# Where the zeros in the unwritten corners of a causal score tile come from: TensorE or ScalarE

## The chip, the cores and the metric

The kernel runs on one core of one Trainium2 chip. The metric is the device time of one execution in microseconds; lower is better. Times come from repeated runs, and views of the profile from one profiled execution of the same kernel.

## The reference, cut to what matters

The reference is a chain of four blocks on x of shape (2, 512, 256), all in float32: causal attention with rotary embedding and 16 heads of 128, a feed-forward block with dequantised weights, a linear attention and a second feed-forward block with weights from a table. The change lies in the first:

```python
attn = jnp.einsum('bihd,bjhd->bhij', q, k) * scale
causal = jnp.triu(jnp.ones((s, s), dtype=bool), k=1)
attn = jnp.where(causal[None, None], -jnp.inf, attn)
attn = jax.nn.softmax(attn, axis=-1)
o = jnp.einsum('bhij,bjhd->bihd', attn, v).reshape(b, s, N_HEADS * D_K)
```

Row i of a head's 512x512 scores has only columns 0 to i. Two sequences of 16 heads make 32 heads.

## The kernel before, in words

**Engines and order.** All instructions of an engine are issued in the order in which the program writes them; the kernel schedules itself. A small planner (`Times` and `Engine`, lines 48 to 187) keeps a model of when each engine is free and when each tile is written. It decides only where side work goes: chains of small steps (`begin` and `poll`, lines 245 to 262), which run whenever TensorE's modelled time `now` has come far enough, and fillers for VectorE (`fill`, line 134). Every operation that goes through `scalar`, `vector`, `pool` or `sync` is recorded at line 183 (DMAs at 165), so the profile shows these lines for nearly everything; tiles tell operations apart. Matrix products go through `matmul` (line 276), which from the first head on cuts an output of 128 rows into two products of 64 rows, one for each half of the array (line 281). Each float32 product leaves two records in the trace, one bfloat16 product one.

**A slot for each head.** `slot(i)` (line 1090) writes, in this order: the scores of head i; the projections of q and k for head i+1; on ScalarE the division of head i's probabilities by their sums; the output projection of head i-2 (`projected_out`); the product of probabilities and values of head i-1 (`attended`, line 983); the turning of head i's probabilities (VectorE transposes and four DMAs into pT, `turned_p`); a part of a later head's values. In the last slots the first feed-forward block takes the place of projections that are no longer needed.

**The scores of a head.** Four tiles of 128 rows, each in two halves of 64 rows (`score_half`, line 933). A half has as many columns as its last row needs, so that the lower half of a tile has 64 columns less than the upper one. Tile 3 (448 and 512 columns) fills a bank of PSUM with the tag "s", tiles 2 and 0 share the next "s" bank, tile 1 (256 and 192 columns) is in a bank with the tag "t". Each tag has two banks, taken in turn (`bank`, line 233). VectorE then reads a whole tile of 128 rows at once with the mask (`scores`, line 911). In tiles 3 and 1 a corner of 64 rows by 64 columns is read that no score is written to: rows 0 to 63 and columns 448 to 511 of tile 3, rows 64 to 127 and columns 192 to 255 of tile 1. The mask makes its values irrelevant, but they must be finite. In tiles 2 and 0 the corners are laid out so that each is a score of the other tile or covered.

**Zeros for the two corners.** `no_scores` (line 949) writes a corner with one bfloat16 product of zeros, 64 columns of weights by 64 columns, taken from the left part of the mask, which is zero. It is called at line 1129, between tile 3 and tile 2, and at line 1145, between the two halves of tile 1.

**The banks of tag "t"** hold tile 1 of a head and `po`, the output of `attended`, which ScalarE then copies with the bias of v to oT (line 996).

Of the kernel before, what the change touches and what calls it, by code (L numbers as in the profile page):

```python
# [19 lines left out]
P = 128  # L20
HALF = P // 2
B = 2
S = 512
# [11 lines left out]
TU = HT * P  # L35
# [155 lines left out]
def sandwich_kernel(  # L191
# [36 lines left out]
    vector, scalar = Engine("DVE", nc.vector, times), Engine("ACT", nc.scalar, times)  # L228
# [4 lines left out]
    def bank(tag):  # L233
        tile = psum.tile([P, 512], F32, tag=tag, name=f"ps_{tag}")
        used = banks.setdefault(tag, deque(maxlen=2))
        if len(used) == 2:
            times.floor[tile.name] = times.end(used[0])
        used.append(tile.name)
        return tile
# [9 lines left out]
    def begin(chain, delay=0.0):  # L249
        chains.append([now[0] + delay, chain])  # L250
# [13 lines left out]
    def catch_up():  # L264
        if behind:
            behind.popleft()()
# [9 lines left out]
    def matmul(out, lhsT, rhs, start, stop, beside=False, **more):  # L276
        m = lhsT.shape[-1]
        step = HALF if halved[0] else P
        for at in range(0, m, step):
            part = slice(at, min(at + step, m))  # L280
            nc.tensor.matmul(out[part], lhsT=lhsT[:, part], rhs=rhs, start=start, stop=stop, **more)  # L281
        now[0] = max(now[0], times.start("PE", [out], [lhsT, rhs]))
        if not beside:
            now[0] += (math.prod(rhs.shape[1:]) / 0.6 + 5) / 1e3
        times.add("PE", now[0], [out], [lhsT, rhs])
# [21 lines left out]
    def col(kind, i):  # L307
        at = {"q": 0, "k": NH, "v": 2 * NH, "g": 3 * NH, "b": 3 * NH + NK}[kind] + i
        return cols_sb[:, at : at + 1]
# [200 lines left out]
    with ExitStack() as at:  # L510
# [57 lines left out]
        mask = ac.tile([P, S + P], F32, name="mask")  # L568
# [259 lines left out]
        NS = B * NH  # L828
# [79 lines left out]
        def blocks(t, n):  # L908
            return t.rearrange("p (b c) -> p b c", c=n)
# [39 lines left out]
        def no_scores(ps):  # L949

            nc.tensor.matmul(ps, lhsT=zeros, rhs=zeros, start=True, stop=True)  # L951

        def exps(i, it):
            p, mn = ps_p[i]
            pi = p[:, p_at[it] : p_at[it] + (it + 1) * P]
            scalar.activation(
                pi,
                pi,
                AF.Exp,
                bias=mn[:, it : it + 1],  # L960
                scale=-1.0,
                accum_out=sums[i][:, it : it + 1],
            )
# [19 lines left out]
        def attended(i):  # L983
            gg, hh = divmod(i, HG)
            po = bank("t")
            for jt in range(NT):
                matmul(
                    po[:, jt * P :],
                    vs[gg][:, jt, hh * DK : (hh + 1) * DK],
                    pT[i][:, :, 4 * jt : 10 + jt : 3, :].rearrange("p i t b -> p t i b"),  # L990
                    jt == 0,
                    jt == NT - 1,
                )
            oT[i] = vp.tile([P, S], F32, tag="oT", name="oT")

            scalar.activation(oT[i], po, AF.Identity, bias=col("v", i % NH))
# [21 lines left out]
        def attention_sums(b):  # L1018
            for t2 in range(NT // 2):
                h = acc[:, 2 * t2 : 2 * t2 + 2, :].rearrange("p t d -> p (t d)")  # L1020
                vector.tensor_add(h, h, yb[b][t2])
# [68 lines left out]
        def slot(i):  # L1090
            b, h = divmod(i, NH)
            g2, odd = divmod(i, HG)
            if i == 0:
                load("q", 2)
            elif i == 2:
                load("k", 2)
            if odd == 0:
                load("v", g2 + 2)
                load("o", g2)
            elif i > 1:  # L1100
                load("q", (i + 3) // 2)
                load("k", (i + 3) // 2)
            if i == 4:
                vector.tensor_tensor(differ, words[:, :, 0], words[:, :, 1], ALU.bitwise_xor)
            if i == NH + 2:
                attention_sums(0)
                begin(after_attention(0))
            if i == NH + 1:

                flat = [  # L1110
                    [t.rearrange("p k c -> p (k c)") for t in (up_i, wu)],
                    [t[0].rearrange("p k s -> p (k s)") for t in (xT0, xTv)],
                ]
                parts = [[t[:, at : at + TU] for at in range(0, t.shape[-1], TU)] for t in flat[1]]
                select_in(
                    parts[0] + parts[1],
                    [tuple(t[:, at : at + TU] for t in flat[0]) for at in range(0, NK * FULL * P, TU)],
                )
            now_in, done = i < NS, not (jobs or behind)
            if now_in:  # L1120
                ps_p[i] = (
                    pr.tile([P, 1280], F32, tag="p", name="p"),
                    small.tile([P, NT], F32, tag="mn", name="mn"),
                )
                sums[i] = small.tile([P, NT], F32, tag="sm", name="sm")
                s3 = bank("s")
                score_half(i, 3, 0, blocks(s3[:, : S - HALF], HALF))
                score_half(i, 3, 1, blocks(s3, HALF))
                no_scores(s3[:HALF, S - HALF :])
                scores(i, 3, blocks(s3, P))  # L1130


                s2 = bank("s")
                ps2 = s2[:, HALF : HALF + 3 * P]
                ps0 = blocks(s2, P)[:, 0:4:3, :HALF]
                score_half(i, 2, 1, blocks(ps2, HALF))
                score_half(i, 2, 0, blocks(ps2[:, : 2 * P + HALF], HALF))
                score_half(i, 0, 0, ps0[:, :1])
                score_half(i, 0, 1, ps0)
                scores(i, 2, blocks(ps2, P))  # L1140
                exps(i, 3)
                scores(i, 0, ps0)
                s1 = bank("t")
                score_half(i, 1, 1, blocks(s1[:, :TU], HALF))
                no_scores(s1[HALF:, TU - HALF : TU])
                score_half(i, 1, 0, blocks(s1[:, : TU - HALF], HALF))
                scores(i, 1, blocks(s1[:, :TU], P))
                exps(i, 2)
                exps(i, 0)
                exps(i, 1)  # L1150
            catch_up()
            if i < NS - 2:
                look_up(i > 0)
            else:
                assert not terms
            turning = []
            for kind in "qk":
                if kind == "q" and i in (0, 2, 3):
                    pass
                elif i + 1 < NS:  # L1160
                    turning.append(projection(kind, i + 1))
                    next(turning[-1])
                    next(turning[-1])
                elif i <= NS:
                    next(main)
                    next(main)
                if kind == "q" and jobs and i % 2 == 0 and i >= 2:
                    dequantised(*jobs.popleft())
                if kind == "q" and i and now_in:
                    inverted(i)  # L1170
            for work in turning:
                next(work, None)
            if now_in:
                p, _ = ps_p[i]
                for it in reversed(range(NT)):
                    pi = p[:, p_at[it] : p_at[it] + (it + 1) * P]
                    scalar.mul(pi, pi, rs[i][:, it : it + 1])
            if 2 <= i < NS + 2:
                projected_out(i - 2)
            if i == 0:  # L1180
                values(0, 1, "t")
            elif i == 1:
                values(1, 1, "t")
            if i in (1, 2):

                ahead = projection("q", i + 2)
                next(ahead)
            if 1 <= i < NS + 1:
                attended(i - 1)
            if i == 0:  # L1190
                values(1, 0)
            if now_in:
                turned_p(i)
            if i in (1, 2):
                for _ in ahead:
                    pass
            poll()
            if i < NS - HG:
                if i > 1:
                    values(i // 2 + 1, odd)  # L1200
            elif i <= NS:
                next(main)
                next(main)
            poll()
            if i < NS - 2:
                look_up(done)
            catch_up()
# [27 lines left out]
        for i in range(NS + 2):  # L1235
            slot(i)
# [313 lines left out]
```

## Time and profile before

| | |
|---|---|
| Median of three runs | 621.93 us (621.89 to 622.28) |
| Profiled execution | 622.14 us |
| its span in the profile | 620.0 us |
| Granted TensorE clock | 1.000 |
| Heads' part of the span (first scores to last scores) | 14.7 to 355.7 us |
| From one head's scores to the next, heads 12 to 30 | 11.04 us |
| Products of zeros | 64 |
| ScalarE busy | 299.6 us, 48% |

The span runs from the first to the last recorded instruction; the execution's own time holds some 2 us around it. PE is TensorE's products and PEld its weight loads, DVE is VectorE, ACT ScalarE, POOL GpSimd, SP SyncE, whose queue issues the DMAs. A row of a group gives the line, the engine, the operation, output and inputs, the shape and how often; then busy time, the mean of one, and the idle time of the engine before them. A row of a timeline gives start, duration, the same names, and how many instructions are merged. `128*64` in a row of TensorE means weights with 64 columns, an output of 64 rows. A product's row includes the time in which its result still runs through the array, so rows of products that follow each other overlap.

### The profile page before, as it was taken

The page shows a single profiled execution, that of the slowest core. Times are in us where ns is not written, and L with a number is a line of the kernel's source. Part 1 is how long each engine was busy: PE and PEld are TensorE (multiplying, and loading weights), DVE is VectorE, ACT ScalarE, POOL GpSimd, SP SyncE. Part 2 cuts the span into 40 slices and gives each one's busy share as a digit, 9 for nine tenths or more (in the row PEclk, how much of TensorE's full clock was granted, in tenths as well). Part 3 has the DMA queues.
Part 4 walks back from the last instruction along what each step waited for, and adds up shares of the span by engine and source line. Part 5 has one row for each costly group of instructions (what it writes and reads, how often), then busy time and mean ns, then how long its engine had stood idle before and what let it go on. Part 6 is the DMA issues. An engine that isn't in the chain of part 4 may idle for free.

```text
span 620.0 us, 13144 instructions
## 1 busy us (share of the span) xinstructions
PE 613.4 (99%) x4938; PEld 433.8 (70%) x4938; DVE 484.1 (78%) x1159; ACT 299.6 (48%) x659; POOL 275.5 (44%) x353
## 2 busy tenths in 40 slices
PE   8999999999999999999999999999999999999996
PEld 6555655555555666667777788888888888886676
DVE  6989988887887999989898888768977562563953
ACT  5646666775556556566556741233232323335130
POOL 5355657354453575755667300440360260261441
PEclk9999999999999999999999999999999999999999
DMA  8567474765547647556452521211000001001010
GB/s 220 143 165 213 105 199 124 170 167 142 162 123 177 169 114 185 154 140 179 110 142 58 131 54 28 108 34 29 2 18 18 2 10 26 1 4 34 19 35 17
DMA packets 43599, 60.90 MB, mean 98 GB/s; under 512 B 5136, under 2 KB 31504, under 8 KB 43536
## 3 DMA queue, kind: packets, MB, share of 16 engines
q1 hardware_dynamic: 43536, 60.07, 37.4%
q8 instruction: 39, 0.64, 0.4%
q14 instruction: 24, 0.20, 0.1%
HBM read 28.33 MB, written 1.05 MB: 47 GB/s over the span
## 4 chain that ended last, share of the span: by engine, by line
PE 98%; DVE 1%; issue 0%; DMA 0%; POOL 0%; ACT 0%; POOLq 0%; DVEq 0%
PE ps_mm L281 40%; PE ps_o L281 22%; PE ps_s L281 21%; PE ps_t L281 15%; DMA x<-in_x 0%; DVE st L183 0%; PE ps_t L288 0%; DVE hT L183 0%; POOLq L1546 0%; POOL rstd L183 0%; DVE mv L183 0%; ACT xT L183 0%; DVE x L183 0%; PE ps_s L288 0%; ACT wu L183 0%
## 5 line engine op out<-in xcount | busy, mean ns | idle before, releaser
L183 DVE SCALAR_TENSOR_TENSOR rr<-ps_mm,cols_sb,sin_sb 64x512 f32<-64x512 f32 (+1 forms) x126 | 93.4, 741 | 3.7 <-PE ps_mm L281 0.9
L183 POOL TENSOR_TENSOR wg<-wg,scratch 128x752 f32<-128x752 f32 x30 | 53.8, 1792 | 90.6 <-DVE scratch L183 88.0
L281 PE MATMUL ps_mm<-xT,wg 128*64 128x256 f32 (+2 forms) x680 | 86.8, 379 | 0.0
L281 PE MATMUL ps_s<-xT,wu 128*64 128x256 f32 (+1 forms) x652 | 82.9, 379 | 0.0
L183 ACT ACTIVATE p<-p,mn 128x512 f32<-128x512 f32 (+3 forms) x128 | 70.3, 550 | 24.6 <-DVE mn L183 24.4
L281 PE MATMUL ps_o<-wd,hT 128*64 128x256 f32 (+2 forms) x680 | 78.5, 376 | 0.0
L281 PE MATMUL ps_t<-pT,v 128*64 128x256 f32 (+3 forms) x512 | 75.5, 433 | 0.0
L281 PEld LDWEIGHTS ps_o<-wd,hT 128*64 128x64 f32 (+1 forms) x680 | 63.0, 141 | 13.2
L281 PEld LDWEIGHTS ps_mm<-xT,wg 128*64 128x64 f32 (+2 forms) x680 | 62.7, 139 | 12.9 <-ACT si L183 0.3
L281 PEld LDWEIGHTS ps_s<-xT,wu 128*64 128x64 f32 (+1 forms) x652 | 60.5, 139 | 12.1 <-DVE hT L183 0.3
L281 PEld LDWEIGHTS ps_t<-pT,v 128*64 128x64 f32 x512 | 45.4, 137 | 31.3 <-issue 22.6
L183 ACT ACTIVATE p<-p,rs 128x512 f32<-128x512 f32 (+3 forms) x128 | 61.4, 551 | 9.7 <-DVE rs L183 7.8
L281 PE MATMUL ps_o<-wo,oT 128*64 128x256 f32 x512 | 61.8, 379 | 0.0
L281 PEld LDWEIGHTS ps_o<-wo,oT 128*64 128x64 f32 x512 | 45.4, 137 | 22.2 <-issue 14.0
L281 PE MATMUL ps_mm<-xT,wq 128*64 128x512 f32 (+2 forms) x252 | 59.8, 583 | 0.4 <-ACT xT L183 0.4
L183 POOL TENSOR_TENSOR ra<-ra,cos_sb 128x512 f32<-128x512 f32 (+1 forms) x33 | 41.0, 1244 | 41.7 <-ACT ra L183 39.1
L281 PE MATMUL ps_mm<-xT,wk 128*64 128x512 f32 x248 | 59.5, 592 | 0.0
L281 PE MATMUL ps_s<-kT,qT 128*64 128x384 f32 (+5 forms) x384 | 57.7, 427 | 0.1
L281 PE MATMUL ps_mm<-wv,xTv 128*64 128x256 f32 x464 | 56.0, 379 | 0.0
L183 DVE STREAM_TRANSPOSE turned<-p 128x512 f32<-128x512 f32 (+3 forms) x128 | 54.1, 480 | 1.9 <-DMA pT<-turned 0.6
L183 ACT ACTIVATE ln<-x,shift,rstd 128x256 f32<-128x256 f32 x24 | 14.9, 626 | 76.7 <-POOL shift L183 76.7
L183 DVE CUSTOM_DVE_ANT_0 p<-ps_s,mask 128x512 f32<-128x512 f32 x64 | 31.1, 486 | 23.1 <-PE ps_s L951 23.1
(155 smaller groups left out, 957.7 us busy)
## 6 DMA issues: line engine op xcount, KB each, us to landing
pT<-turned SPq DMA_DIRECT2D x128, 208.0 KB, 3.9
wo<-in_wo SPq DMA_DIRECT2D x17, 256.0 KB, 4.0
wv<-in_wv SPq DMA_DIRECT2D x16, 256.0 KB, 4.0
wq<-in_wq SPq DMA_DIRECT2D x15, 256.0 KB, 4.7
wk<-in_wk SPq DMA_DIRECT2D x15, 256.0 KB, 4.5
xT<-tr SPq DMA_DIRECT2D x44, 64.0 KB, 2.2
pk_g<-in_gate_p SPq DMA_DIRECT2D x4, 256.0 KB, 4.3
sc_g<-in_gate_s SPq DMA_DIRECT2D x8, 128.0 KB, 4.0
```

What stands on the lines that cost most here:

```text
L183: return write(*args, **more)
L281: nc.tensor.matmul(out[part], lhsT=lhsT[:, part], rhs=rhs, start=start, stop=stop, **more)
```

## The change

For heads 2 to 30 the two products of zeros are left out. Instead a new function `prepare` takes the head's first "s" bank and its "t" bank early, in the slot before, and ScalarE copies zeros from the mask into the two corners. It is called from `attended`, behind its products and ahead of ScalarE's oT: `attended(i)` is written in slot i+1 and prepares head i+2. Heads 0, 1 and 31 keep the products. Since each bank is the next that its tag would give, the banks of all tiles are the same as before.

```diff
+        prepared = {}
+
+        def prepare(i):
+
+            prepared[i] = bank("s"), bank("t")
+            for rows, cs, ps in (
+                (slice(0, HALF), slice(S - HALF, S), prepared[i][0]),
+                (slice(HALF, P), slice(TU - HALF, TU), prepared[i][1]),
+            ):
+                scalar.copy(ps[rows, cs], mask[rows, :HALF])
+
@@ attended
+
+            if i + 2 < NS - 1:
+                prepare(i + 2)
             oT[i] = vp.tile([P, S], F32, tag="oT", name="oT")
 
             scalar.activation(oT[i], po, AF.Identity, bias=col("v", i % NH))
@@ slot
-                s3 = bank("s")
+                ready = prepared.pop(i, None)
+                s3 = ready[0] if ready else bank("s")
                 score_half(i, 3, 0, blocks(s3[:, : S - HALF], HALF))
                 score_half(i, 3, 1, blocks(s3, HALF))
-                no_scores(s3[:HALF, S - HALF :])
+                if not ready:
+                    no_scores(s3[:HALF, S - HALF :])
                 scores(i, 3, blocks(s3, P))
...
-                s1 = bank("t")
+                s1 = ready[1] if ready else bank("t")
                 score_half(i, 1, 1, blocks(s1[:, :TU], HALF))
-                no_scores(s1[HALF:, TU - HALF : TU])
+                if not ready:
+                    no_scores(s1[HALF:, TU - HALF : TU])
                 score_half(i, 1, 0, blocks(s1[:, : TU - HALF], HALF))
                 scores(i, 1, blocks(s1[:, :TU], P))
```

The planner records the copies as work of ScalarE, as it does every operation; the products of zeros it did not count. So the places that it chooses for side work behind the heads can change too.

## The prediction, made before the changed kernel was run

> **What bounds the kernel now.** I read the page's busy line and the chain that ended last first, then the groups of TensorE by shape, then the timeline of one head on TensorE and on ScalarE, and last the end of TensorE's timeline.
>
> ```profile
> span 620.0 us, 13144 instructions
> ...
> PE 613.4 (99%) x4938; PEld 433.8 (70%) x4938; DVE 484.1 (78%) x1159; ACT 299.6 (48%) x659; POOL 275.5 (44%) x353
> ...
> PE 98%; DVE 1%; issue 0%; DMA 0%; POOL 0%; ACT 0%; POOLq 0%; DVEq 0%
> ```
>
> TensorE is busy in 99% of the span and is 98% of the chain. The view of waits has it waiting for other engines only in the first microseconds (1.0, 0.4 and 0.2 us). Its clock is granted in full. So what leaves TensorE's queue shortens the kernel, and what other engines get costs only if TensorE comes to wait for it.
>
> The groups by shape (columns: count, busy us, mean ns of one, idle):
>
> ```profile
> L281 PE MATMUL ps_s<-kT,qT 128*64 128x384 f32 x64 | 26.9, 501 | 0.1
> L281 PE MATMUL ps_s<-kT,qT 128*64 128x320 f32 x64 | 22.5, 433 | 0.0
> ...
> L281 PE MATMUL ps_t<-kT,qT 128*64 128x256 f32 x64 | 19.1, 380 | 0.0
> L281 PE MATMUL ps_t<-kT,qT 128*64 128x192 f32 x64 | 16.6, 341 | 0.0
> ...
> L951 PE MATMUL ps_t<-mask 128*64 128x64 bf16 x32 | 6.2, 193 | 0.0
> L951 PE MATMUL ps_s<-mask 128*64 128x64 bf16 x32 | 6.2, 192 | 0.0
> ```
>
> The zeros are 64 products of 193 ns, 12.4 us in the busy column, but that is not their price: products overlap. One row lasts about 167 ns plus its columns: 433 for 320 and 380 for 256 differ by 53 ns for 64 columns, 0.83 ns a column. The price is the distance between starts. Two shapes break the line: 384 columns should take 433 + 53 = 486 and take 501; 192 should take 380 - 53 = 327 and take 341. These two follow a product of zeros. Each float32 product leaves two records, and only the first comes right behind the zeros, so 14.5 ns in the mean is 29 ns in that one.
>
> One head, TensorE (start, duration):
>
> ```profile
> 141.91 1.02 PE L281 MATMUL ps_s<-kT,qT 128*64 128x512 f32 x4
> 142.66 0.19 PE L951 MATMUL ps_s<-mask 128*64 128x64 bf16 x1
> 142.69 0.99 PE L281 MATMUL ps_s<-kT,qT 128*64 128x384 f32 x8
> 143.48 0.38 PE L281 MATMUL ps_t<-kT,qT 128*64 128x256 f32 x1
> 143.52 0.19 PE L951 MATMUL ps_t<-mask 128*64 128x64 bf16 x1
> 143.55 0.53 PE L281 MATMUL ps_t<-kT,qT 128*64 128x192 f32 x3
> 143.90 1.89 PE L281 MATMUL ps_mm<-xT,wq 128*64 128x512 f32 x8
> ```
>
> Products of 64 output rows go side by side into two halves of the array. The scores of this head last from 141.906 to 143.904 (the trace's own starts), 1.998 us; all heads 2 to 30 show 1.998 to 2.004. The lower half has 448+384+64+256 columns, the upper 512+320+128+192: 1152 each, twice, at 0.833 ns: 1.920 us, and some 2.5 ns for each of eight products: 1.940. The excess is 0.058 us, and each half has one product of zeros. So neither half hides the other's.
>
> **What it removes.** Behind the last 448 columns the zeros start at 142.662 and the next product at 142.690: 28 ns. That product's weights began to load only when the zeros began (142.664), the load behind it began at 142.720, and so its own took 56 ns, of which the zeros covered 28; the rest is the 29 ns seen in the groups. In the other half it is the same (143.521, 143.549, 143.579). Price: 28 + 29 = 57 ns in each half, once in a head, halves in parallel. The Trainium skill (TensorE: Matmul & The Clock Gate, "Wait — 56ns, not 53.3ns?") speaks against this much: a small matmul costs its floor, start to start about 25 ns. By that a head gains 25 ns and 29 heads 0.73 us, lost within what can be told from no change; by the rows it is more than twice that, because the floor leaves out the weight load that a 28 ns product is too short to cover. I take the rows, as the excess of 58 ns confirms them. The function that prepares is called for heads 2 to 30, 29 heads (0, 1 and 31 keep the products): 29 x 57 = 1.65 us, all on the path.
>
> **What it adds on ScalarE.** Two copies of 64x64 in 29 heads. The nearest row is the copy of v, 128x512 at 585 ns; less 448 columns at 0.83 it is 212 ns. Bounds: 187 ns, the engine's smallest row (reading an accumulator), and 387 ns, the scaling of 128x128. Two take 0.42 us by my value, 0.37 to 0.77 by the bounds. They stand behind the four scalings of p and ahead of oT:
>
> ```profile
> 137.82 1.92 ACT L183 ACTIVATE p<-p,rs 128x512 f32<-128x512 f32 x4 [0.55 <-DVE rs L183]
> 140.40 0.69 ACT L183 ACTIVATE oT<-ps_t,cols_sb 128x512 f32<-128x512 f32 x1 [0.66 <-PE ps_t L281]
> ```
>
> ScalarE sits idle ahead of oT for 0.63 to 1.3 us in nearly every head from 4 on (0.41 in head 20). So the copies fill that hole; at 0.77 us oT would be 0.1 us late in every second head, and oT is read only in the next slot, behind its scores and projections; the copy of v behind oT has a hole of its own (1.04 us here). No cost. Without that cover 0.42 us would go into the exponentials, whose products have room too: in this head pT lands at 146.60 and is read at 149.06; the room is 1.4 us in the first three heads and 2.3 or more after.
>
> **The new waits.** The first product of scores of a head waits for the first copy. The scalings end 1.88 to 4.1 us before that product in all these heads (139.74 to 141.91 here), so 0.42 us of copies leave 1.4 us or more. The banks rotate as before, and the copies wait for no other engine in the build. In front of the product of 256 columns the build puts one more semaphore instruction on TensorE's queue; nothing but the rest of the scores and q's projection is queued behind it. Two such instructions in a row start 111 ns apart (146.510, 146.621). But they run ahead of the array: the one for the scores at 139.986, 1.92 us early, the one for q's projection at 141.507, 2.40 us early. I take nothing; the bound is 111 ns in each head. VectorE's readers of two of the four banks get a second wait, at most 0.1 us each, where VectorE idles for 0.8 to 2.35 us before the first (heads 10 to 12); its work behind (exponentials, turning, pT) has the room named above. Nothing.
>
> **What it moves.** The kernel's planner counts ScalarE's copies, so work after the heads is placed a little differently. Comparing the two builds: q, k, v of the first token pair come 8 products earlier, of the second 8 later, of the third 16 later, with their output products 4, 8 and 16 later; of the last pair 12 earlier, its output 8 earlier. A group of 8 products takes 1.73 us. TensorE's work is the same, so only stalls count. SyncE's and GpSimdE's instructions only follow these chains. The dangerous one is the last pair: 12 products are 2.6 us, so q, k, v would start at 563.0 instead of 565.6, while their input's last transfer is issued at 562.3 now and lands some 2.2 us later (the median of these transfers). But the feed-forward sum that feeds it also ends 8 products earlier (1.73 us), and the normalisation that stood ahead of its own on VectorE (that of the third pair) is now behind it. The same chain took 13.7 us in the first pair, where nothing was ahead: 546.5 + 13.7 = 560.2, 2.8 us in time. A stall that exists now may go: at the end
>
> ```profile
> 594.13 2.76 PE L281 MATMUL ps_o<-wd,hT 128*64 128x256 f32 x24
> 596.83 0.88 PE L288 MATMUL ps_t<-ident,ln 128*128 128x128 f32 x4
> 597.54 2.76 PE L281 MATMUL ps_o<-wd,hT 128*128 128x256 f32 x12
> ```
>
> 24 records at 0.108 are over at 596.72, and the four transposes take 0.71 instead of 4 x 0.107: TensorE waits about 0.32 us for ln. The new order has 40 products (8.6 us) where 36 (7.8 us) stood between the last output product and the transposes, against a chain of 8.1 us (from the output's end at 588.96 to that of ln at 597.10). Bounds for the moves: -0.4 (this stall and one of 0.1 us at 557.8 gone) and +1.5 us (the last pair's input as late as now). I take -0.15, half of that one stall.
>
> **Sum.** -1.65 - 0.15 = -1.80 us. The profiled execution took 622.14 (span 620.0 and 2.1 around it), so 620.34; it stands 0.21 above the median of 621.93, so 620.1 for a median.
>
> **The rivals.**
> - *The end gives it back* (0.12). The new order makes TensorE wait where nothing waited: worst at the last pair, +1.5 us; with 1.0 us taken the time is 621.93 - 1.65 + 1.0 = 621.3. For: 1.1 us was the room there and the move is 2.6. Against: what feeds it moves too.
> - *Only the floor is saved* (0.07): the weights of the product after next turn out to be the limit, 25 ns a head, 621.93 - 0.73 = 621.2. For: the scores have the shortest products of the kernel (64 columns, 53 ns, against a load of 56). Against: both halves' excess adds up to 58.
> - *Slower* (0.11): the semaphore instruction in front of the 256 columns holds the array. Price 111 ns x 29 = 3.2 us, less 1.65: 621.93 + 1.57 = 623.5. It decides once the queue's lead at that place is below 0.11 us. For: the scores have the most instructions in the least time, and the wait for a copy (about 140.0 to 140.2) now holds the queue just before. Against: 1.7 us of products are still queued then, and a wait of 1.3 us at 146.621 held nothing up.
>
> **How the numbers follow.** The likeliest, 620.1, has 0.70; its own range is 619.4 (all stalls of the end gone and 0.3 us of small gaps besides) to 620.6. Adding the first two rivals up to 621.6 leaves out about 0.15. A measurement of this kernel tells 0.2%, 1.24 us, from no change: the likeliest is faster, the first two rivals are within, the third is slower: 0.70, 0.19, 0.11.
>
> **What would show it.** Scores of 1.94 us in heads 2 to 30, their period shorter by 0.057; 384 and 192 columns at 487 and 327 ns mean; six records of zeros left; copies of about 0.21 us in the hole before oT. It is wrong if TensorE's rows name ScalarE as releaser, if the scores keep 1.97 or more, or if TensorE stands still between 420 and 600 us.

## The result and the profile after

The changed kernel takes 620.12 us (median, 619.97 to 620.48), the kernel before on the same chip 622.11: ratio 0.9968, interval 0.9959 to 0.9977. That is 2.0 us less. The profiled execution's span is 618.1 us, the granted clock full.

The page of the changed kernel, busy line and chain:

```profile
span 618.1 us, 13150 instructions
...
PE 611.0 (99%) x4876; PEld 397.7 (64%) x4876; DVE 483.3 (78%) x1159; ACT 312.0 (50%) x717; POOL 275.9 (45%) x353
...
PE 96%; DVE 2%; issue 1%; DMA 0%; POOL 0%; ACT 0%; POOLq 0%; DVEq 0%
```

TensorE still bounds it. Its busy column fell by 2.4 us and its weight loads' by 36.1 us, and neither figure is the saving. ScalarE gained 12.4 us of busy time, and its share of the chain stays 0%.

The groups by shape, TensorE's and then ScalarE's copies (count, busy us, mean ns, idle):

```profile
L281 PE MATMUL ps_s<-kT,qT 128*64 128x384 f32 x64 | 26.0, 488 | 0.1
...
L281 PE MATMUL ps_t<-kT,qT 128*64 128x192 f32 x64 | 15.7, 327 | 0.0
...
L951 PE MATMUL ps_t<-mask 128*64 128x64 bf16 x3 | 0.6, 193 | 0.0
L951 PE MATMUL ps_s<-mask 128*64 128x64 bf16 x3 | 0.6, 192 | 0.0
```

```profile
L183 ACT COPY ps_t<-mask 64x64 f32<-64x64 f32 x29 | 6.1, 212 | 0.7
L183 ACT COPY ps_s<-mask 64x64 f32<-64x64 f32 x29 | 6.1, 209 | 0.7
```

The two shapes that stood off the line are back on it (501 to 488, 341 to 327 ns), those of 320 and 256 columns did not move (433, 380), and six records of zeros are left. One head on TensorE, then its ScalarE a little earlier:

```profile
141.11 1.78 PE L281 MATMUL ps_s<-kT,qT 128*64 128x512 f32 x12
142.63 0.60 PE L281 MATMUL ps_t<-kT,qT 128*64 128x256 f32 x4
143.05 1.46 PE L281 MATMUL ps_mm<-xT,wq 128*64 128x512 f32 x6
```

```profile
137.09 1.92 ACT L183 ACTIVATE p<-p,rs 128x512 f32<-128x512 f32 x4 [0.61 <-DVE rs L183]
139.03 0.21 ACT L183 COPY ps_s<-mask 64x64 f32<-64x64 f32 x1
139.26 0.21 ACT L183 COPY ps_t<-mask 64x64 f32<-64x64 f32 x1
139.61 0.69 ACT L183 ACTIVATE oT<-ps_t,cols_sb 128x512 f32<-128x512 f32 x1
```

The scores run from 141.11 to 143.05 without a product of zeros between them. The copies fill most of the hole that stood ahead of oT. By the trace's own starts the scores of heads 2 to 30 last 1.942 us in the mean (1.940 to 1.945) where they lasted 2.000.

Stage by stage, from the same starts:

| us | before | after | difference |
|---|---|---|---|
| start to head 0's scores | 14.66 | 14.52 | -0.15 |
| head 0 to head 2 | 18.46 | 18.46 | 0.00 |
| head 2 to head 31 | 320.24 | 318.73 | -1.51 |
| head 31 to the end | 266.61 | 266.41 | -0.20 |

The heads should have given 29 x 0.058 = 1.68. In head 14's slot TensorE has a new stall of 0.24 us ahead of the products of pT (at 170.36), and an older stall of 0.06 is gone: -1.68 + 0.24 - 0.06 = -1.50. At the end, where four transposes took 0.71 us before:

```profile
594.32 0.66 PE L288 MATMUL ps_t<-ident,ln 128*128 128x128 f32 x4
594.81 2.54 PE L281 MATMUL ps_o<-wd,hT 128*128 128x256 f32 x11
```

The first record starts at 594.32 and the next product at 594.81, 0.49 us for the four; by the starts of the records TensorE waits 0.10 us ahead of them, where it waited 0.10 there and 0.22 among them. Two smaller stalls change places: 0.10 us ahead of the product at 557.80 in the kernel before is gone, and 0.09 ahead of the one at 434.38 is new.

### The profile page after: what moved, and what is told of

Same layout as the page of the kernel before. It is cut to its first block, busy times and chain, and to the rows that moved or that the text cites. A ratio compares the mean times of both kernels' runs of the same rounds, so it can differ in the third digit from the quotient of the medians.

```text
span 618.1 us, 13150 instructions
## 1 busy us (share of the span) xinstructions
PE 611.0 (99%) x4876; PEld 397.7 (64%) x4876; DVE 483.3 (78%) x1159; ACT 312.0 (50%) x717; POOL 275.9 (45%) x353
## 4 chain that ended last, share of the span: by engine, by line
PE 96%; DVE 2%; issue 1%; DMA 0%; POOL 0%; ACT 0%; POOLq 0%; DVEq 0%
PE ps_mm L281 39%; PE ps_o L281 22%; PE ps_s L281 21%; PE ps_t L281 14%; DVE rr L183 0%; DMA x<-in_x 0%; DVE turned L183 0%; DVE st L183 0%; DVE wu L183 0%; DVE xTv L183 0%; DVE xT L183 0%; DVE ra L183 0%; DVE hT L183 0%; POOLq L1563 0%; PE ps_t L288 0%
## 5 line engine op out<-in xcount | busy, mean ns | idle before, releaser
L281 PEld LDWEIGHTS ps_mm<-xT,wg 128*64 128x64 f32 (+2 forms) x680 | 56.5, 139 | 19.1 <-ACT ge L183 0.3
L281 PEld LDWEIGHTS ps_o<-wd,hT 128*64 128x64 f32 (+1 forms) x676 | 55.5, 141 | 20.7
L281 PEld LDWEIGHTS ps_s<-xT,wu 128*64 128x64 f32 (+1 forms) x652 | 54.4, 139 | 18.1 <-DVE hT L183 0.3
L281 PEld LDWEIGHTS ps_t<-pT,v 128*64 128x64 f32 x512 | 42.0, 137 | 34.8 <-issue 25.5
L281 PEld LDWEIGHTS ps_o<-wo,oT 128*64 128x64 f32 x512 | 42.5, 137 | 25.2 <-issue 15.1
L281 PE MATMUL ps_s<-kT,qT 128*64 128x64 f32 (+5 forms) x384 | 57.4, 425 | 0.1
L183 DVE TENSOR_TENSOR hT<-ge,ps_s 128x512 f32<-128x512 f32 x32 | 21.8, 684 | 41.6 <-ACT ge L183 22.9
L281 PEld LDWEIGHTS ps_s<-kT,qT 128*64 128x64 f32 x384 | 34.3, 137 | 24.2 <-issue 7.5
```

The costliest lines, as they stand in the source:

```text
L183: return write(*args, **more)
```

## The experiments

Each question takes one step of the prediction; the rivals are in the expectations. All times stand beside runs of the kernel before on the same chip (622.0 to 622.3 in each case).

**Is the price a weight load that isn't covered?** The products of zeros of the kernel before are made wider, N = 64, 128 and 256 columns. The one for the s bank has to stand ahead of the 448 columns then, so the first of the three only moves it.

```diff
+no_scores(s3[:HALF, S - N :])
 score_half(i, 3, 0, blocks(s3[:, : S - HALF], HALF))
 score_half(i, 3, 1, blocks(s3, HALF))
-no_scores(s3[:HALF, S - HALF :])
...
-no_scores(s1[HALF:, TU - HALF : TU])
+no_scores(s1[HALF:, TU - N : TU])
```

> The kernel before, with the product of zeros of the s bank moved ahead of the 448 columns (still 64 columns wide): the control for the two wider ones, where it has to stand there because the 448 columns overwrite a part of it. Theory: place does not matter, the price is 28 ns of its own and 29 of the next product's weight load: scores 2.00 us, time as before, 622.1. Rival (the price came from standing between two particular products): scores differ from 2.00 by more than 0.02.

> Both products of zeros made 128 columns wide in place of 64, ahead of the products that overwrite the other half of them. Theory (behind a 64-column product of zeros 29 ns of the next weight load of 56 ns lie open): 128 columns last some 54 ns and cover the load, so the price stays at 56 to 57 ns though the work doubles: scores 2.00 us, time as before, 622.1; the product behind loses its extra 29 ns. Rival one (29 ns is a fixed price of a product of zeros, for its change of type or its drain): 54 + 29 = 83 ns, scores 2.027, time 32 x 0.027 = 0.85 above, 622.95. Rival two (a floor of 25 ns and no more): would have shown 1.97 before.

> Both products of zeros 256 columns wide. Theory: 256 columns at 0.42 ns are 107 ns and cover the load wholly; price 107 to 109 ns in each half: scores 2.05 us, time 32 x 0.051 = 1.6 above the kernel before, 623.75. Rival one (fixed 29 ns on top): 136 ns, scores 2.08, time 2.55 above, 624.65.

Measured: 622.34, 622.22 and 623.70 us; ratios 1.0004 (0.9995 to 1.0012), 1.0003 (0.9995 to 1.0012), 1.0028 (1.0017 to 1.0040). Scores: 2.001, 2.001, 2.051 us in the mean of heads 2 to 30. The groups with 128 columns of zeros, then with 256 (with 64 these two are as before, 341 and 193 ns, and the 448 columns behind the moved zeros take 554):

```profile
L281 PE MATMUL ps_s<-kT,qT 128*64 128x448 f32 x64 | 29.4, 541 | 0.0
...
L281 PE MATMUL ps_t<-kT,qT 128*64 128x192 f32 x64 | 15.7, 327 | 0.0
...
L951 PE MATMUL ps_s<-mask 128*64 128x128 bf16 x32 | 7.0, 219 | 0.0
```

```profile
L281 PE MATMUL ps_s<-kT,qT 128*64 128x448 f32 x64 | 29.3, 539 | 0.0
...
L281 PE MATMUL ps_t<-kT,qT 128*64 128x192 f32 x64 | 15.6, 326 | 0.0
...
L951 PE MATMUL ps_s<-mask 128*64 128x256 bf16 x32 | 8.7, 273 | 0.0
```

Twice the columns cost nothing: what the zeros take longer, the product behind takes less (192 columns go from 341 to 327; the 448, which now follow the other zeros, from 554 to 541). Only when the load is covered, from 128 to 256 columns, does the width count: 50 ns in a head for 128 columns of 0.42 ns (53; the rows of the zeros grow from 219 to 273 ns). No fixed 29 ns on top is left. Moving the zeros moved the excess from the 384 columns to the 448 and changed no time.

**Does one half hide the other's product?** ScalarE writes one of the two corners only.

```diff
 for rows, cs, ps in (
     (slice(0, HALF), slice(S - HALF, S), prepared[i][0]),
-    (slice(HALF, P), slice(TU - HALF, TU), prepared[i][1]),
 ):
...
-if not ready:
-    no_scores(s1[HALF:, TU - HALF : TU])
+no_scores(s1[HALF:, TU - HALF : TU])
```

> ScalarE writes zeros for the corner of the s bank only; the product of zeros for the t bank stays in every head. The s corner lies in the lower half of the array, the t corner in the upper. Theory of the prediction (the two halves work side by side, each zero product costs its own half 57 ns, and the longer half sets the head): nothing is gained, scores of heads 2 to 30 stay at 2.00 us, the time is that of the changed kernel plus 29 x 0.057 = 1.65, some 621.8 us. Rival one (the products share one price, half of it each): scores 1.971 us, time 0.83 above the changed kernel, some 620.95. Rival two (the s product carried all of it): scores 1.942 and the time of the changed kernel, 620.1.

> The other corner alone: ScalarE writes zeros for the t bank, the product of zeros for the s bank stays. Theory of the prediction (halves side by side, the longer one sets the head): scores stay at 2.00 us, the time is some 621.8 us. Rival one (half the price each): scores 1.971, 620.95 us. Rival two (the t product carried all of it): scores 1.942, 620.1 us.

(The second kernel is the mirror of this diff.) Measured: 621.96 us, ratio 0.9997 (0.9988 to 1.0006), and 621.66 us, ratio 0.9996 (0.9987 to 1.0005). Neither gains anything that can be told from nothing; both together gain 2.0. Both rivals fall. From head 2 to head 31 it takes 320.16 and 320.11 us, against 320.24 and 318.73.

The period of a head in the trace says more (from one head's first product of scores to the next's; "5" is from head 5 to head 6):

```text
head             5       7       9      10      11      13      14      15      20      22      29
before      11.043  11.043  11.044  11.043  11.039  11.039  11.038  11.039  11.038  11.039  11.039
after       10.985  10.985  10.985  10.985  10.981  10.980  11.219  10.985  10.980  10.980  10.980
s corner    10.985  10.985  10.985  11.020  11.038  11.038  11.682  10.985  10.985  11.038  11.037
t corner    10.980  11.043  11.043  11.043  11.044  11.043  11.044  11.043  11.044  11.043  11.043
```

Without the zeros of the s corner the head costs 10.985 up to head 9 and 11.038 from head 11; a stall at head 14 sets it back to 10.985 for seven heads. So the half without zeros pulls ahead by 0.05 us a head (0.04 at the start of head 4's scores, 0.36 at head 10's) until it has 0.38 us there and 0.43 at their end, and from then on it goes no further ahead. The heads that looked free only build a lead, and the stall, where both halves wait for the same data, takes it: this slot is 0.70 us longer than the next. Without the zeros of the t corner the other half leads, and there the lead stops growing at 0.16 us, in head 6. One of the long leads, on TensorE of the kernel with the s corner alone:

```profile
263.82 0.54 PE L281 MATMUL ps_s<-kT,qT 128*64 128x448 f32 x1
...
264.20 1.56 PE L281 MATMUL ps_s<-kT,qT 128*64 128x512 f32 x9
...
265.77 0.59 PE L281 MATMUL ps_mm<-xT,wq 128*64 128x512 f32 x1
265.81 0.19 PE L951 MATMUL ps_t<-mask 128*64 128x64 bf16 x1
```

The lower half begins the scores 0.38 us before the upper, which is still at a product of v (263.98); at the end it starts q's projection at 265.77, before the zeros and the 192 columns (265.84) that stand ahead of it in the queue. What caps the lead at 0.43 us on one side and at 0.16 on the other was not tried.

**Does the planner's order pay at the end?** The copies are issued past the planner.

```diff
-scalar.copy(ps[rows, cs], mask[rows, :HALF])
+nc.scalar.copy(ps[rows, cs], mask[rows, :HALF])
```

> The changed kernel with its copies issued so that the planner does not count them: TensorE's order of products is that of the kernel before throughout, also behind the heads. Theory (0.24 us of the gain came from behind the heads, where the new order waits less for the last transposes): scores 1.942 us as in the changed kernel, from the start of head 31's scores to the end 266.64 us as before, and a time 0.24 above the changed kernel, some 620.35 us. Rival (the tail differed by chance between two executions, not by the order): the tail is 266.40 and the time that of the changed kernel, 620.1.

Measured: 620.52 us, ratio 0.9974 (0.9965 to 0.9983). The times of the two orders overlap, the profiles don't. From head 31 to the end: 266.59 to 266.64 us in the five kernels with the old order (before, this one, the three with wider zeros), 266.36 to 266.50 in six with the new one (after, its second profile, and four of the others). The kernel with the s corner alone has the new order and 266.71, but its halves meet at head 31 with a stall of 0.62 us, where the others have 0.3 or a little less. So the order is worth 0.2 us behind the heads. It is the second wait of the four transposes, which this kernel has again: they take 0.71 to 0.73 us in the five and 0.49 in all seven with the new order. From head 2 to the end, though, this kernel's profile takes 585.09 us and that of the changed kernel 585.14, as only the second has the stall in head 14's slot.

**Where do free copies end?** The same zeros are written four times, then eight times.

```diff
-scalar.copy(ps[rows, cs], mask[rows, :HALF])
+for _ in range(4):
+    scalar.copy(ps[rows, cs], mask[rows, :HALF])
```

> The changed kernel with every copy of zeros made four times: 8 copies of 0.21 us in a head, 1.69 us on ScalarE in place of 0.42, where the hole ahead of oT is 0.63 to 1.3 us. Theory (ScalarE's work is off the path, and behind oT there is another hole of about 1 us): oT ends 0.4 to 1.1 us later, no row of TensorE waits for it, scores 1.94 us, time within 0.3 of the changed kernel. Rival (the copies cost nothing only as long as they fit the hole; beyond it they push the exponentials, and through pT the products behind): TensorE waits for pT or oT in most heads, some 0.4 to 1.0 us each, 12 to 29 us in all.

> The changed kernel with every copy of zeros made eight times: 16 copies in a head at 0.235 us from start to start, 3.75 us on ScalarE in place of 0.47. Theory (the copies are free only as long as holes take them): with 8 copies oT, v's copy and the exponentials already stood about 1 us later in a head with other copies beside them, and pT's room is 0.2 to 2 us; 1.9 us more uses that up, TensorE waits for pT in most heads, 0.5 to 1 us each, 13 to 29 us in all: 633 to 649 us. Rival (ScalarE, 50% busy, takes any of it): time within 0.5 us of the changed kernel, 620.1.

Measured: 620.11 us, ratio 0.9969 (0.9958 to 0.9981), and 642.43 us, ratio 1.0327 (1.0313 to 1.0341). ScalarE with four, in the head shown above:

```profile
140.66 0.94 ACT L183 COPY ps_t<-mask 64x64 f32<-64x64 f32 x4
141.63 0.69 ACT L183 ACTIVATE oT<-ps_t,cols_sb 128x512 f32<-128x512 f32 x1
```

The eight copies take from 139.71 to 141.60, 1.9 us. By the distance from the scalings (137.76 here), oT stands 1.3 us further back (0.9 in every other head), and nothing comes late of it: from head 2 to head 31 it takes 318.48 us. With eight, around one of the largest waits, first ScalarE, then TensorE:

```profile
76.81 1.90 ACT L183 COPY ps_s<-mask 64x64 f32<-64x64 f32 x8
78.73 1.91 ACT L183 COPY ps_t<-mask 64x64 f32<-64x64 f32 x8
```

```profile
78.81 1.83 PE L281 MATMUL ps_s<-kT,qT 128*64 128x448 f32 x12 [2.18 <-POOL kT L183]
80.69 0.65 PE L281 MATMUL ps_t<-kT,qT 128*64 128x256 f32 x4
```

The row names kT, but kT was done at 78.00. The copies into the s bank end at 78.71, and the scores start 0.10 us later; those into the t bank end at 80.64, and the 256 columns start 0.05 us later. It is the same in all seven heads where TensorE stands idle for over 0.5 us ahead of the scores: these start 0.10 us behind the copies. A late pT shows in one row of the waits alone (0.4 us). So the size was as expected, and the way was another: the scores wait for the copies themselves. Of 23.2 us between the two spans, 17.8 are lost from head 2 to head 31 and 4.8 behind the heads, where no zeros are written: the planner counts 16 copies a head and places its work anew. That part was not tried apart.

**Do heads 0 and 1 give the same?** Their zeros come from ScalarE too, head 1's behind head 0's scalings and the copy of v.

```diff
+prepare(0)
 project("q", 1, "o")
...
     values(0, 1, "t")
+    prepare(1)
```

> The changed kernel with the zeros of heads 0 and 1 written by ScalarE too, so that only head 31 keeps its products. Theory: the same price in these heads, 2 x 0.058 = 0.12 us less, 620.0 us, within what a measurement can tell from the changed kernel; the scores of heads 0 and 1 go from 2.022 and 2.025 to 1.96 to 1.97, where they are not set by a wait for q. Rival: these two heads wait for other things (k and q are not there yet), so the time of their scores stays and nothing is gained.

Measured: 623.83 us, ratio 1.0022 (1.0012 to 1.0032): 3.7 us worse than the changed kernel. ScalarE and TensorE around head 1:

```profile
21.32 1.92 ACT L183 ACTIVATE p<-p,rs 128x512 f32<-128x512 f32 x4 [1.15 <-DVE rs L183]
...
23.72 0.21 ACT L183 COPY ps_s<-mask 64x64 f32<-64x64 f32 x1
```

```profile
24.03 2.91 PE L281 MATMUL ps_s<-kT,qT 128*64 128x448 f32 x11 [2.10 <-ACT ps_s L183]
```

The same copy of 0.21 us, behind other work, holds TensorE for 2.1 us. In the later head shown above the copies end at 139.47 and the first scores come 1.6 us behind them. And in this run the wait costs more than itself. By windows (us; busy us of TensorE, weight loads, VectorE, ScalarE, GpSimdE; granted clock, DMA share and GB/s):

```profile
24.00:26.00 2.00, 1.97 (x8) 1.27 (x10) 0.19 (x1) 0.68 (x2) 0.00 (x0) 0.60 0.38 47
26.00:28.00 2.00, 2.00 (x14) 1.56 (x12) 1.32 (x7) 1.02 (x3) 0.00 (x0) 0.54 0.96 208
```

The granted clock is 0.60 and 0.54 in these four microseconds, and 1.00 ahead of them and behind; the scores of head 1 take 3.49 us. From head 0 to head 2 it takes 22.10 us in place of 18.46, which is nearly the whole loss.

Not every run of this kernel lost the clock. Some 3.4 us at half of it, as these two rows add up to, leave a mean of 0.997 over the span. Five of the nine runs have 0.995 to 0.997 and take 623.83 to 624.28 us; three have 1.000 and take 622.56, 622.60 and 623.26; the ninth has 0.998 and takes 622.99. So the place alone costs some 2.4 to 3.1 us, and the lost clock 1.0 to 1.5 us more.

The next kernel puts head 1's copies ahead of the scalings:

```diff
     values(0, 1, "t")
-    prepare(1)
...
+if i == 0:
+    prepare(1)
 if now_in:
     p, _ = ps_p[i]
```

> As the kernel that prepares heads 0 and 1 too, but head 1's two copies stand ahead of the four scalings of head 0 in ScalarE's queue, in its hole of 1.15 us, not behind them and behind the copy of v. Theory (the 3.7 us that kernel lost came from TensorE's wait of 2.1 us for these copies, and from half its clock for some 3.4 us behind that wait): the wait is gone, scores of head 1 are back at about 2 us, granted clock full, time 620.0, at most 0.1 better than the changed kernel. Rival (the loss comes from preparing heads 0 and 1 at all, for instance from the copies in the start): the time stays near 623.8.

Measured: 620.80 us, ratio 0.9978 (0.9967 to 0.9988). The clock and the scores are back (1.945 us in head 1), so most of the 3.7 us came from the place:

```profile
22.00:26.00 4.00, 4.00 (x32) 2.23 (x30) 3.79 (x13) 3.80 (x11) 0.00 (x0) 1.00 0.62 151
```

But the 0.1 us expected over the changed kernel is not there. The t banks now go round in another order:

```profile
PE ps_t L281 <- DVE mn L183: 0.5, 1, 0.5
```

A product of v waits until VectorE has read head 0's bank; from head 0 to head 2 it takes 18.81 us, 0.35 more than in the changed kernel. No version here beats that one.

**Was the stall at head 14 chance?** The changed kernel once more.

> The changed kernel once more, beside the other on one chip. Theory (the 0.24 us by which the slot of head 14 was longer in its first profile came from one late transfer of pT, not from the change): this profile's stalls for pT are elsewhere or nowhere, from head 2's scores to head 31's it takes 318.5 us, not 318.73; time 620.1. Rival (the change itself brings pT of head 13 late): the same slot is 0.2 longer again.

Measured: 620.05 us, ratio 0.9964 (0.9950 to 0.9977). The slot of head 14 is long again, 11.325 us, and another 0.09 to 0.12 us for pT is lost in head 3's: 318.96 us from head 2 to 31, not 318.5. That expectation failed. It isn't that pT leaves late. SyncE's queue in the changed kernel:

```profile
162.35 3.31 SPq L165 DMA_DIRECT2D pT<-turned  x4
165.71 0.60 SPq L165 DMA_DIRECT2D wv<-in_wv  x1
```

pT is issued 10.26 us after its head's start, as before (10.27), but takes 7.96 us to its last part where it took 6.52; the weights of the next pair go out close behind it, as they did before. The stall is there in both profiles of the changed kernel and in the kernel with the s corner alone, and in none of the others that write zeros by ScalarE, the one with eight copies aside, where so much is late. But such a stall doesn't need ScalarE's zeros. In the kernel with 128 columns of zeros, where ScalarE writes none, pT of head 25 takes 8.13 us and TensorE waits for it: the slot of head 26 is 0.30 us longer. In the kernel before, the same transfer takes 7.69 us and leaves 0.21. So a slow transfer of pT is no mark of the change. Why head 13's is slow in these three stays open.

## Why the prediction was right

- *TensorE bounds it, so what leaves its queue counts.* Right.
- *57 ns a head.* Right: 58 ns in the scores, 1.68 us in 29 heads against 1.65. The kernels with wider zeros show the cause, a load left uncovered. The floor of 25 ns alone, the second rival, would have left 1.97 us for the scores; they are 1.942. The distance of two starts is short here too (28 ns); it just isn't the price.
- *Neither half hides the other's.* Right over a whole run, shown by removing one at a time. The prediction did not see that a half can lead for some heads, and in these the period is the short one.
- *Copies of 212 ns that cost nothing.* Right: 209 and 212 ns, in the hole before oT, and four times as many cost nothing still. At eight times the cover is gone.
- *The semaphore instruction before the 256 columns.* Nothing, as taken. It stands in every one of the heads whose scores last 1.940 to 1.945, as long as the 1.940 that the prediction worked out without it. The slower rival falls.
- *The moves at the end, -0.15.* Right in place: -0.20. The wait of the transposes that was named shrank from 0.32 to 0.10, and the other one named (0.1 at 557.8) went, but one of 0.09 came at 434.4, between 420 and 600 us, where none was expected. To take half of the first was a guess, and that the two smaller ones nearly cancel was luck. The last pair's input was in time, so the first rival falls.
- *"The room is 1.4 us in the first three heads and 2.3 or more after".* Wrong. A transfer reports its landing in 16 parts, and the working had read the first. By the last part the room before is 0.25 to 0.42 us in heads 0 to 2 and 0.21 to 2.1 in heads 3 to 29; after, it is 0.04 in head 13, and TensorE waits. The step "its products have room too" stood on this figure. It did no harm, as the copies never needed the room, but it is where 0.24 us of the gain went.

The sum of -1.80 us met -1.99 in the medians and -1.86 in the two spans. The spans hold a start that is 14.5 to 15.5 us long from one profile to the next, whatever the kernel, so such a difference is no finding. That the sum fits so well is in part luck: the new stall of 0.24 us, which it did not have, is offset in these two spans by an older one of 0.06 gone and a start shorter by 0.15. The heads' own term, 1.68 against 1.65, is no luck.

## What to carry to other kernels

A short product costs its own time and what it leaves open of the next weight load; look for shapes behind it that are longer than their columns, and don't count the busy column. Where two halves of the array work side by side, take the same from both or gain nothing. A copy on an engine with holes is free only in its place: read what stands ahead of it in that queue when TensorE is ready, since the same 0.21 us cost nothing in 29 heads and over 2 us in one, more where the clock fell too.

## What was not expected of the hardware

TensorE's wait of 2.10 us for head 1's copies was followed by some 3.4 us at half its clock (0.60 and 0.54 in the four microseconds behind it, above). The wait alone doesn't decide it: in three of nine runs of that kernel the mean clock was 1.000. Nor did a wait of 2.18 us ahead of 78.81 with eight copies bring it:

```profile
78.80:80.00 1.20, 1.19 (x8) 0.80 (x10) 1.13 (x7) 1.04 (x6) 0.55 (x1) 1.00 0.48 57
80.00:82.00 2.00, 1.95 (x17) 1.20 (x15) 2.00 (x6) 1.91 (x6) 0.00 (x0) 1.00 0.91 171
```

The Trainium skill (TensorE: Matmul & The Clock Gate, "HAM oscillation — how this bites in real kernels") asks to avoid idle gaps above some 3.4 us; by head 1's rows a shorter one can do. What decides it was not tried.

The two halves of the array don't keep step: one was up to 0.43 us ahead in the kernel with the s corner alone, and began a product (265.77) before two of the other half that stood ahead of it in the queue (265.81 and 265.84).
